# The front of layer 2: transposes one group ahead, score turns behind them, later additions on GpSimd

## The chip, the core and the metric

The kernel runs on one core of a Trainium2 chip. The core has five engines that matter here: PE (TensorE: matrix products and transposes), DVE (VectorE), ACT (ScalarE), POOL (GpSimd) and SP (SyncE, which here only issues DMAs). Each engine works through its own list of instructions in order; an instruction that waits holds up all that stand behind it in the same list. Engines wait for each other by semaphores. The metric is the device time of one execution in microseconds (us).

## What is computed

Four layers follow each other. Each adds a graph network and then a feed-forward network to `x`, an array of 2708 rows (nodes) and 256 columns in float32. The change lies at the seam between layer 1's feed-forward network and layer 2's graph network, which in the reference reads, cut to what matters:

```python
x = x + _L1_ffn_ref(...)                       # layer 1 ends
# layer 2, graph attention on the normalised rows
h = x @ W.T
a_src = (h * attn_src).sum(axis=-1)
a_dst = (h * attn_dst).sum(axis=-1)
scores = a_src[None, :] + a_dst[:, None]
mask = (adj > 0).astype(h.dtype)
s = jnp.where(scores > 0, scores, ALPHA * scores) * mask      # ALPHA = 0.2
e = jnp.exp(s - max) * mask
w = e / (e.sum(axis=1) + 1e-08)
out = elu(w @ h)
```

The kernel uses that exp of the leaky score is the larger of two products. It scales row j of `h` by exp(a_src[j]) and keeps that factor as a 257th column (together `hh`), and it needs one row of exp(0.8 a_dst) laid over all partitions (`Rb`) and one column exp(-0.8 a_src) (`G`). An element of the attention matrix is then max(Rb, G) times the mask.

## The kernel before, in words

The 2708 rows are 21 tiles of 128 and one of 20. `FOURS` splits them into six groups: one of two tiles, then five of four (the last has three full tiles and the one of 20).

Layer 1's feed-forward network has left its result in device memory (`given[1]`), written there row by row by indirect DMAs. The front of layer 2 does this for each group, with the lines of the profile:

1. SP loads the group's rows of that result into the tile `mine` (L56 in `load_tiles`; L61 for the 20 rows). `mine` has two buffers, so the third load may be issued only when the first group's additions have read theirs, and so on. Each load is 512 KB for a group of four.
2. DVE adds `mine` to `x`, two tiles at a time (L1413, 128x512).
3. PE transposes each tile of `x` in two halves into PSUM (L213 in `turn_to`), and ACT copies them to the tile `xT4` (L214, 128x256, one copy per tile). `ps_tmp` has three PSUM banks.
4. DVE takes mean and variance of each row (L186 `bn_stats`, L187), ACT makes 1/sqrt of it by logarithm and exponential (L141, `var`). The mean needs no subtraction, since the weights were centred.
5. PE multiplies by the weights and the two attention vectors (L260, 258 columns, one PSUM bank per tile; `ps_acc` has five banks).
6. ACT scales the two score columns into `sc` (L1425); GpSimd has cleared `sc` before (L1421).
7. The row scores are turned from a column to a row: a transpose on PE (L1342), a copy on ACT (L1344), a write to device memory by SP (L1345), a read by SP that lays the row over all partitions (L1349, into `Rb`), and an exponential on ACT (L141 on `Rb`). This is the round trip of the scores.
8. ACT makes the other exponentials (L141: the 257th column of `hh`, `G`, `rowe`), and DVE scales the products from PSUM into `hh` (L1433), which also frees the five `ps_acc` banks.

Behind the front comes the attention loop (L1494 on DVE makes the elements `e`, in four buffers; L1502 on PE multiplies them with `hh`). DVE makes the first four `e` while the front still runs. After each diagonal tile of `e` has been read, GpSimd copies a block into `mask` (L1781).

The order on each engine is not written out by hand here. The framework under the kernel takes the order of the calls and the dependences and puts the instructions of neighbouring groups into each engine's list as it sees fit; each engine then keeps to its list. What the engines' lists look like after the change can be read from the built program.

Of the kernel before, what the change touches and what calls it, by code (L numbers as in the profile page):

```python
# [8 lines left out]
F32 = mybir.dt.float32  # L9
# [27 lines left out]
def rows(t):  # L37
    return min(P, N - t * P)
# [8 lines left out]
FOURS = [range(0, 2)] + [range(t, min(t + 4, NT)) for t in range(2, NT, 4)]  # L47
# [19 lines left out]
def adj_ffn4(ctx: ExitStack, tc: tile.TileContext, a: dict, out: bass.AP):  # L67
# [72 lines left out]
    def lnexp(out, in_, func, **kw):  # L140
        i = s.activation(out, in_, func, **kw)  # L141
        tc.add_manual_dep(i.ins, pinned[-1].ins.name, mybir.DependencyInfo(
            mybir.DependencyClass.NoSync, mybir.DependencyReason.DATA), reason="table")
# [33 lines left out]
    def stats(tiles, src=None, by_log=False):  # L177


        G = len(tiles)  # L180
        mv = small.tile([P, G, 2], F32, name="mv", tag=f"mv{G}", bufs=2)
        v.memset(mv[:, G - 1, :], 1.0)
        for i, t in enumerate(tiles):
            r = rows(t)
            st = small.tile([P, 6], F32, name="st")
            v.bn_stats(st[:r], x[:r, t, :] if src is None else src[:r, i, :])  # L186
            v.bn_aggr(mv[:r, i, :], st[:r])  # L187
        var = small.tile([P, G], F32, name="var", tag=f"var{G}", bufs=2)
        if by_log:
            lnexp(var, mv[:, :, 1], AF.Ln, bias=eps)  # L190
            lnexp(var, var, AF.Exp, scale=-0.5)
            return mv, var
        v.tensor_scalar(var, mv[:, :, 1], EPS, None, op0=ALU.add)
        return mv, rsqrt(small, var, G)
# [14 lines left out]
    def turn_to(xT, xn, r, bank=None):  # L209

        p = ps_tmp() if bank is None else bank
        for c in range(DC):
            te.transpose(p[:, c * P : c * P + r], xn[:, c * P : (c + 1) * P], ident[:r, :r])  # L213
        s.copy(xT, p[:, : DC * P].rearrange("p (c t) -> p c t", c=DC)[:, :, :r])  # L214
# [297 lines left out]
    def behind(i, past):  # L512
        for p in past:
            tc.add_manual_dep(i.ins, p.name, mybir.DependencyInfo(
                mybir.DependencyClass.Sync, mybir.DependencyReason.DATA), reason="scattered rows")
# [822 lines left out]
    def row_scores(kept, scores, t0, n):  # L1338


        p = ps_tmp()
        te.transpose(p[:n, :P], scores, ident)  # L1342
        er = w_l1[:n, 0, :P]
        s.copy(er, p[:n, :P])  # L1344
        nc.sync.dma_start(kept.rearrange("t h c -> (t h) c")[t0 : t0 + n, :], er)  # L1345
# [16 lines left out]
    with tc.tile_pool(name="t3", reuse_waits="tile", bufs=1) as t3:  # L1362
# [34 lines left out]
        with tc.tile_pool(name="g2", reuse_waits="tile", bufs=1) as gp:  # L1397
# [2 lines left out]
            rowe = gp.tile([P, NT, 1], F32, name="rowe")  # L1400
            Rb = gp.tile([P, NT * P], F32, name="Rb")
            kept = tc.dram_tile([NT, 1, P], F32, name="rows2")
            for tiles in FOURS:
                n, t0 = len(tiles), tiles[0]
                o = gp.tile([P, 4, D], F32, name="mine", bufs=2)
                for i in load_tiles(nc, o, tiles, given[1], t0):
                    behind(i, scattered["given1"])
                for k in range(0, n, 2):
                    for q, m in (((P, 2),) if rows(t0 + k + 1) == P else
                                 ((P, 1), (rows(t0 + k + 1), 1))):  # L1410
                        i = k if q == P else k + 1
                        xs = x[:q, t0 + i : t0 + i + m, :]
                        v.tensor_tensor(xs, xs, o[:q, i : i + m, :], ALU.add)  # L1413
                xT = gp.tile([P, DC, W], F32, name="xT4", bufs=2)
                own = tiles_of(t0 * P, (n - 1) * P + rows(tiles[-1]))
                for t, k, r in own:
                    turn_to(xT[:, :, k : k + r], x[:r, t, :], r)
                rstd = stats(tiles, by_log=True)[1]

                sc = gp.tile([P, 4, 2], F32, name="sc", bufs=2)  # L1420
                g.memset(sc, 0.0)  # L1421
                ps = []
                for i, (t, k, r) in enumerate(own):
                    ps.append(times(xT, k, r, w_l2, D + 2, ps_acc()))
                    s.activation(sc[:r, i, :], ps[-1][:, D:], AF.Copy, scale=rstd[:r, i : i + 1])  # L1425
                row_scores(kept, sc[:, :n, 1], t0, n)
                row_factor(Rb[:, t0 * P : (t0 + n) * P], kept, 0, t0, n)
                lnexp(hh[:, t0 : t0 + n, D], sc[:, :n, 0], AF.Exp)
                lnexp(G[:, t0 : t0 + n, 0], sc[:, :n, 0], AF.Exp, scale=-0.8)

                lnexp(rowe[:, t0 : t0 + n, 0], sc[:, :n, 1], AF.Exp, scale=-0.2, bias=ln8)
                for i, (p, (t, k, r)) in enumerate(zip(ps, own)):
                    v.tensor_scalar(hh[:r, t, :D], p[:, :D], rstd[:r, i : i + 1], hh[:r, t, D :],  # L1433
                                    op0=ALU.mult, op1=ALU.mult)

            spread_out(hh[:, FULL, :])
            spread_out(G[:, FULL, :])
# [593 lines left out]
```

## Time and profile before

| | us |
|---|---|
| median of four runs shown | 1925.19 (1918.24 to 1929.15) |
| the profiled execution | 1930.74 |
| its span, first instruction to last | 1929.0 |
| of it: up to the first load of `mine` | 1103.62 |
| layer 2's front, to the first product of the attention loop | 36.36 (PE busy 29.11, DVE 27.52, ACT 19.08, POOL 2.88) |
| attention loop, to 1355 | 215.02 (PE busy 211.02, DVE 115.84) |
| the rest | 574.00 (PE busy 550.88) |

The profile comes from one execution. A timeline row gives the start in us, the length, the engine, the line in the kernel, the operation, the names of what is written and read, the shapes, how many equal instructions were put together, and in brackets how long the engine stood idle before it and what ended that. `PEld` rows are weight loads, which run beside the products. A group row gives the busy time, the mean length of one in ns, and the idle time before the group with its releasers. The chain of waits follows the work that ended last back from the end: each row is a start, a length, and what the time went to. "issue" is time in which the profile shows no wait.

### The profile page before, as it was taken

To read this page: it belongs to the slowest core of one execution; us is meant where nothing else is said; L and a number is where in the kernel's file an instruction comes from. 1 tells how busy PE (TensorE), PEld (TensorE's weight loads), DVE (VectorE), ACT (ScalarE), POOL (GpSimd) and SP (SyncE) were. 2 spreads that over 40 slices of the span, in tenths; PEclk is the share of its full clock that TensorE was granted. 3 is DMA by queue.
4 is the path that set the end of the run, shared out by engine and by line. 5 is a ranking of instruction groups with operands and counts; after the bars stand their busy time and mean duration, and the time that the engine had idled before them with its cause. 6 is when DMAs were issued, how large, how long until landed. Compare 5 with 4: busy or idle time off the path is not lost.

```text
span 1929.0 us, 25747 instructions
## 1 busy us (share of the span) xinstructions
PE 1832.0 (95%) x9453; PEld 1328.7 (69%) x9453; DVE 1100.7 (57%) x2498; ACT 643.1 (33%) x1459; POOL 343.2 (18%) x406
## 2 busy tenths in 40 slices
PE   7999998999999999999989699999899999999998
PEld 6888787888888888887778578888557732232344
DVE  7777861443433625344532175555354398999897
ACT  7868741222222303113222142222232552031131
POOL 1004254333322001303356300000000000000000
PEclk9999998999998999999999999999899999999999
DMA  8435655887773554544679620000101000000000
GB/s 274 137 112 162 218 187 214 316 331 276 279 290 104 171 151 118 150 114 131 201 246 341 226 68 1 1 1 1 44 1 33 17 1 23 23 12 28 20 20 15
DMA packets 90142, 243.94 MB, mean 126 GB/s; under 512 B 18160, under 2 KB 44824, under 8 KB 80793
## 3 DMA queue, kind: packets, MB, share of 16 engines
q1 hardware_dynamic: 73048, 199.80, 30.7%
q0 software_dynamic: 16960, 42.42, 6.9%
q8 instruction: 78, 1.28, 0.3%
q14 instruction: 56, 0.45, 0.1%
HBM read 216.29 MB, written 28.71 MB: 127 GB/s over the span
## 4 chain that ended last, share of the span: by engine, by line
PE 39%; DMA 4%; DVE 2%; ACT 2%; issue 2%; POOL 1%; another core or an unknown queue 0%; POOLq 0%; SPq 0%; DVEq 0%; ACTq 0%
PE num L1929 10%; PE ps_acc L1502 9%; PE den L1939 6%; PE ps_tmp L367 4%; PE ps_acc L1692 3%; PE ps_tmp L260 2%; DMA L_ffn_beta<-in_L_ffn_beta 1%; PE yacc L719 1%; PE ps_acc L260 1%; DMA names<-taken,b_ix 1%; DMA given<-ys,names 1%; PE ps_tmp L213 1%; DVE e L1899 1%; DMA wb<-in_L_ffn_Wdp 0%; DMA taken<-names,r_ix 0%
## 5 line engine op out<-in xcount | busy, mean ns | idle before, releaser
L1899 DVE SCALAR_TENSOR_TENSOR e<-arena,G,mask 128x1024 f32<-128x1024 f32 (+1 forms) x264 | 287.0, 1148 | 13.7 <-PE den L1939 13.6
L1929 PE MATMUL num<-e,wh 128*64 128x512 f32 (+4 forms) x1056 | 215.7, 551 | 0.0
L1502 PE MATMUL ps_acc<-hh,e 128*128 128x257 f32 x882 | 199.3, 382 | 1.9 <-ACT o L1445 1.9
L1290 PE MATMUL acc<-sup,adrow 128*128 128x256 f32 x882 | 200.8, 385 | 0.3 <-DVE adrow L1258 0.3
L929 PE MATMUL acc<-msg,wt 128*128 128x256 f32 x882 | 198.1, 381 | 2.8 <-DVE x L954 1.6
L1290 PEld LDWEIGHTS acc<-sup,adrow 128*128 128x128 f32 x882 | 167.1, 192 | 28.8 <-issue 5.9
L929 PEld LDWEIGHTS acc<-msg,wt 128*128 128x128 f32 x882 | 165.2, 190 | 28.7 <-DVE x L954 2.3
L1502 PEld LDWEIGHTS ps_acc<-hh,e 128*128 128x128 f32 x882 | 163.7, 190 | 29.5 <-ACT o L1445 4.5
L617 PE MATMUL yacc<-wb,hTs 128*128 128x256 f32 x736 | 171.4, 385 | 6.6 <-DVE ys L619 3.8
L583 PE MATMUL ps_acc<-xTs,wa 128*128 128x256 f32 (+1 forms) x768 | 171.4, 376 | 4.9 <-DVE xTs L573 3.8
L585 ACT ACTIVATE hTs<-ps_acc,wa 128x256 f32<-128x256 f32 (+1 forms) x192 | 88.9, 465 | 247.8 <-PE yacc L617 167.4
L583 PEld LDWEIGHTS ps_acc<-xTs,wa 128*128 128x128 f32 x768 | 137.5, 191 | 32.2 <-DVE xTs L573 7.4
L617 PEld LDWEIGHTS yacc<-wb,hTs 128*128 128x128 f32 x736 | 138.8, 193 | 26.3 <-DVE ys L619 5.0
L1929 PEld LDWEIGHTS num<-e,wh 128*64 128x64 f32 (+1 forms) x1056 | 66.5, 136 | 127.3 <-issue 105.6
L1494 DVE SCALAR_TENSOR_TENSOR e<-Rb,G,mask 128x640 f32<-128x640 f32 (+2 forms) x110 | 85.0, 773 | 90.6 <-PE ps_acc L1502 90.4
L1939 PE MATMUL den<-e,wh 128*32 128x512 f32 (+4 forms) x1056 | 118.0, 548 | 0.0
L214 ACT COPY xT<-ps_tmp 128x256 f32<-128x256 f32 x98 | 33.7, 365 | 240.4 <-PE ps_tmp L213 218.6
L1255 DVE TENSOR_SCALAR mask<-adrow 128x1024 uint8<-128x1024 f32 (+1 forms) x66 | 41.5, 629 | 123.3 <-DMA adrow<-in_adjT 122.6
L719 PE MATMUL yacc<-wb,hTs 128*128 128x256 f32 x384 | 89.6, 387 | 10.5 <-DMA wb<-in_L_ffn_Wdp 8.1
L719 PEld LDWEIGHTS yacc<-wb,hTs 128*128 128x128 f32 x384 | 72.6, 194 | 21.7 <-issue 9.6
L887 DVE SCALAR_TENSOR_TENSOR wt<-adrow,wt 128x640 f32<-128x640 f32 (+3 forms) x67 | 71.1, 1063 | 28.0 <-ACT wt L141 23.9
L1939 PEld LDWEIGHTS den<-e,wh 128*32 128x32 f32 (+1 forms) x1056 | 30.2, 108 | 77.9 <-issue 73.8
(457 smaller groups left out, 2565.9 us busy)
## 6 DMA issues: line engine op xcount, KB each, us to landing
adhalf<-in_adjT SPq DMA_DIRECT2D x42, 677.0 KB
wb<-in_L_ffn_W2p SPq DMA_DIRECT2D x24, 1152.0 KB
wb<-in_L_ffn_Wdp SPq DMA_DIRECT2D x24, 1152.0 KB
wa<-in_L_ffn_W1b SPq DMA_DIRECT2D x24, 1028.0 KB
adrow<-in_adjT SPq DMA_DIRECT2D x42, 512.0 KB
adrow<-in_adjT SPq DMA_DIRECT2D x42, 320.0 KB
adrow<-in_adjT SPq DMA_DIRECT2D x21, 576.0 KB
adrow<-in_adjT SPq DMA_DIRECT2D x21, 448.0 KB
```

Of the source, the lines that this page charges most:

```text
L367: te.matmul(p[:, :w], lhsT=w1[:, c, f * P : (f + 1) * P], rhs=xnT[:, c, c0 : c0 + w], start=(c == 0), stop=(c == DC - 1))
L583: i = te.matmul(p[:, f % 2, : m * P], lhsT=w1[:, c, f * P : (f + 1) * P], rhs=xT[:, c, : m * P], start=(c == 0), stop=(c == DC - 1))
L585: s.activation(hT[:, f, : m * P], p[:, f % 2, : m * P], AF.Gelu, bias=bias[:, f : f + 1])
L617: te.matmul(q[:, k, :], lhsT=hT[:, f, k * P : (k + 1) * P], rhs=w2[:, f, :], start=(f == 0), stop=(f == HC - 1))
L719: te.matmul(q, lhsT=hT[:, f, :], rhs=w2[:, f, :], start=(f == 0), stop=(f == HC - 1))
L929: te.matmul(p[:q, n - pair[0], :], lhsT=wt[:, k : k + q], rhs=msg[:r, j, :], start=(j == 0 and n == pair[0]), stop=(j == FULL - 1 and n == ...
L1290: te.matmul(p[:q, n - pair[0], :], lhsT=ad[:, k : k + q], rhs=sup[:, jj, :], start=(jj == 0 and n == pair[0]), stop=(jj == FULL - 1 and n ...
L1494: i = v.scalar_tensor_tensor(e[:r, :w], Rb[:r, c0 : c0 + w], G[:r, j, :], mask[:r, j, c0 : c0 + w], op0=ALU.max, op1=ALU.mult)
L1502: te.matmul(p[:, : D + 1], lhsT=e[:, k : k + q], rhs=hh[:, j, :], start=(j == 0), stop=False)
L1899: v.scalar_tensor_tensor(e[:, :w], slow[:, m % 2, k, :w], G[:, j, 2 * pair + k, :], mask[:, j, c0 : c0 + w], op0=ALU.max, op1=ALU.mult)
L1929: te.matmul(num[k * DK : (k + 1) * DK, hf, :q], lhsT=wh[some, j, 2 * pair + k, :DK], rhs=e[some, h0 - c0 : h0 - c0 + q], start=(j == 0), s ...
L1939: te.matmul(den[z : z + Q, :q], lhsT=wh[some, i, 2 * pair + k, DK : DK + 1] .to_broadcast([some.stop - some.start, Q]), rhs=e[some, h0 - c ...
```

## The change

The loop over the groups is split in two functions and run one group out of step.

`turned_up(tiles)` does steps 1 to 4 of a group: load, addition, transposes, copies, statistics. It differs in three things. Two tiles are transposed into one PSUM bank, so that one copy of 128x512 takes the place of two of 128x256. A pair is transposed right after its own addition. And from the third group on the additions are given to GpSimd (`adder`).

`valued(tiles, xT, rstd)` does steps 5, 6 and 8: products, score columns, exponentials, `hh`. The `hh` products are called ahead of two of the exponentials.

The loop at the end calls `turned_up` of the next group behind `valued` of the present one, so that the transposes of group k + 2 are called ahead of the products of group k + 1, and calls the score turns (`row_scores`, `row_factor`, step 7) behind those transposes. The first pass fills two groups.

```diff
-            for tiles in FOURS:
+
+            def turned_up(tiles):
+
                 n, t0 = len(tiles), tiles[0]
+                adder = v if t0 < FOURS[2][0] else g
                 o = gp.tile([P, 4, D], F32, name="mine", bufs=2)
                 for i in load_tiles(nc, o, tiles, given[1], t0):
                     behind(i, scattered["given1"])
+                xT = gp.tile([P, DC, W], F32, name="xT4", bufs=2)
                 for k in range(0, n, 2):
...
-                        v.tensor_tensor(xs, xs, o[:q, i : i + m, :], ALU.add)
-                xT = gp.tile([P, DC, W], F32, name="xT4", bufs=2)
+                        adder.tensor_tensor(xs, xs, o[:q, i : i + m, :], ALU.add)
+                    p = ps_tmp()
+                    for i in range(2):
+                        q = rows(t0 + k + i)
+                        for c in range(DC):
+                            te.transpose(p[:, (c * 2 + i) * P : (c * 2 + i) * P + q],
+                                         x[:q, t0 + k + i, c * P : (c + 1) * P], ident[:q, :q])
+                    s.copy(xT[:, :, k * P : (k + 1) * P + r],
+                           p.rearrange("p (c t) -> p c t", c=DC)[:, :, : P + r])
+                return tiles, xT, stats(tiles, by_log=True)[1]
+
+            def valued(tiles, xT, rstd):
+
+                n, t0 = len(tiles), tiles[0]
                 own = tiles_of(t0 * P, (n - 1) * P + rows(tiles[-1]))
-                for t, k, r in own:
-                    turn_to(xT[:, :, k : k + r], x[:r, t, :], r)
-                rstd = stats(tiles, by_log=True)[1]
...
-                row_scores(kept, sc[:, :n, 1], t0, n)
-                row_factor(Rb[:, t0 * P : (t0 + n) * P], kept, 0, t0, n)
                 lnexp(hh[:, t0 : t0 + n, D], sc[:, :n, 0], AF.Exp)
...
+                return sc, t0, n
+
+            ahead, todo = [turned_up(FOURS[0])], list(FOURS[1:])
+            for k in range(len(FOURS)):
+                sc, t0, n = valued(*ahead.pop(0))
+                while todo and len(ahead) < 2:
+                    ahead.append(turned_up(todo.pop(0)))
+                    if len(ahead) == 1:
+                        row_scores(kept, sc[:, :n, 1], t0, n)
+                if k > 0:
+                    row_scores(kept, sc[:, :n, 1], t0, n)
+                row_factor(Rb[:, t0 * P : (t0 + n) * P], kept, 0, t0, n)
```

Nothing else in the program changes. In the attention loop DVE's list has one `e` placed one step later; on the other engines the lists behind the front are the same.

More of the change, by code (lines that the diff above doesn't have):

```diff
@@ L1407, in adj_ffn4 @@
                     behind(i, scattered["given1"])
+                xT = gp.tile([P, DC, W], F32, name="xT4", bufs=2)
                 for k in range(0, n, 2):
-                    for q, m in (((P, 2),) if rows(t0 + k + 1) == P else
-                                 ((P, 1), (rows(t0 + k + 1), 1))):
+                    r = rows(t0 + k + 1)
+                    for q, m in (((P, 2),) if r == P else ((P, 1), (r, 1))):
                         i = k if q == P else k + 1
                         xs = x[:q, t0 + i : t0 + i + m, :]
-                        v.tensor_tensor(xs, xs, o[:q, i : i + m, :], ALU.add)
-                xT = gp.tile([P, DC, W], F32, name="xT4", bufs=2)
+                        adder.tensor_tensor(xs, xs, o[:q, i : i + m, :], ALU.add)
[10 more added lines that the diff above has]
+                n, t0 = len(tiles), tiles[0]
                 own = tiles_of(t0 * P, (n - 1) * P + rows(tiles[-1]))
-                for t, k, r in own:
-                    turn_to(xT[:, :, k : k + r], x[:r, t, :], r)
-                rstd = stats(tiles, by_log=True)[1]
                 sc = gp.tile([P, 4, 2], F32, name="sc", bufs=2)
@@ L1425, in adj_ffn4 @@
                     s.activation(sc[:r, i, :], ps[-1][:, D:], AF.Copy, scale=rstd[:r, i : i + 1])
-                row_scores(kept, sc[:, :n, 1], t0, n)
-                row_factor(Rb[:, t0 * P : (t0 + n) * P], kept, 0, t0, n)
                 lnexp(hh[:, t0 : t0 + n, D], sc[:, :n, 0], AF.Exp)
-                lnexp(G[:, t0 : t0 + n, 0], sc[:, :n, 0], AF.Exp, scale=-0.8)
-                lnexp(rowe[:, t0 : t0 + n, 0], sc[:, :n, 1], AF.Exp, scale=-0.2, bias=ln8)
                 for i, (p, (t, k, r)) in enumerate(zip(ps, own)):
@@ L1434, in adj_ffn4 @@
                                     op0=ALU.mult, op1=ALU.mult)
+                lnexp(G[:, t0 : t0 + n, 0], sc[:, :n, 0], AF.Exp, scale=-0.8)
+                lnexp(rowe[:, t0 : t0 + n, 0], sc[:, :n, 1], AF.Exp, scale=-0.2, bias=ln8)
+                return sc, t0, n
[9 more added lines that the diff above has]
+                row_factor(Rb[:, t0 * P : (t0 + n) * P], kept, 0, t0, n)
             spread_out(hh[:, FULL, :])
```

## The prediction

> **What bounds the kernel now.** I read the page first, then the chain of waits from 1100 us, then each engine's timeline there. On the page PE is busy 95% of the span; a stretch matters only where PE stands still in it. The changed stretch, layer 2's front, runs from the first load of `mine` (1103.62) to the first product of the attention loop (1139.98): 36.36 us, in which PE is busy 29.11, DVE 27.52, ACT 19.08. In the loop behind it PE is busy 211.02 of 215.02 us, so what the front loses or gains is passed on whole.
>
> ```profile
> span 1929.0 us, 25747 instructions
> ```
>
> The chain, start, length, what:
>
> ```profile
> 1103.62 2.66 DMA mine<-given
> ...
> 1113.26 3.50 PE ps_acc L260 x16
> ...
> 1117.78 2.70 DMA rows<-L_gnn_W
> 1120.50 3.24 DMA Rb<-rows
> 1123.73 0.02 issue
> 1123.76 0.63 ACT Rb L141
> 1124.39 0.27 ACT xT L214
> 1124.65 0.04 issue
> 1124.70 0.44 PE ps_tmp L213 x2
> ```
>
> See that a row-score round trip (write, read back, exponential) gets on the chain, because ACT's queue holds the next group's xT copies behind it. PE's timeline shows the same place and the small waits of every group (idle before, and releaser, in brackets):
>
> ```profile
> 1118.42 3.65 PE L260 MATMUL ps_acc<-w_l,xT 128*128 128x258 f32 x16
> 1122.51 0.27 PE L1342 MATMUL ps_tmp<-ident,sc 128*4 128x128 f32 x1 [0.44 <-ACT sc L1425]
> 1122.62 0.94 PE L213 MATMUL ps_tmp<-ident,x 128*128 128x128 f32 x6
> 1124.70 0.44 PE L213 MATMUL ps_tmp<-ident,x 128*128 128x128 f32 x2 [1.14 <-ACT xT L214]
> 1139.98 0.70 PE L1502 MATMUL ps_acc<-hh,e 128*128 128x257 f32 x2
> ```
>
> The rows that price what is added, from the groups of GpSimd and the timelines of GpSimd and DVE:
>
> ```profile
> L1821 POOL TENSOR_TENSOR x<-x,L_gnn_b 128x256 f32<-128x256 f32 x5 | 3.5, 721 | 368.1 <-PE ps_tmp L260 366.9 <-DVE st L186 1.2
> 1128.30 0.95 POOL L1781 COPY mask<-diag 128x128 uint8<-128x128 uint8 x1 [5.25 <-DVE e L1494]
> 1130.13 0.29 POOL L1781 COPY mask<-diag 128x128 uint8<-128x128 uint8 x1
> 1128.26 0.84 DVE L1494 SCALAR_TENSOR_TENSOR e<-Rb,G,mask 128x640 f32<-128x640 f32 x1
> 1110.74 0.69 DVE L1413 TENSOR_TENSOR x<-x,mine 128x512 f32<-128x512 f32 x1
> ```
>
> **The change, part by part.** I take prices from rows and walk them along the order in which the built program of the changed kernel lists each engine's instructions. The same walk over the kernel before puts its first loop product at 1140.1; the trace says 1139.98.
>
> *Transposes one group ahead, turns of the scores behind them.* The work of PE is the same: per group of four, 8 transposes 1.13 us (1117.30 to 1118.42), 16 product passes of 0.2175 = 3.48, one score turn 0.13. What goes are the waits: 0.44 before each of five score turns (ACT's last `sc`), and 1.14, 0.20 and 0.21 for xT copies. PE's own work sets a floor: first transposes 1107.06 to 1108.17 (clock 0.50 until 1110.25 in the windows); then, new, one transpose of the second group stands ahead of the first products and waits for DVE's add (1107.94 + 0.65), so the products start at 1108.95, three passes at half clock, five at full: 1111.3; seven transposes and the turn: 1112.45; here PE waits until about 1113 for ACT, which does eight small operations before it copies xT; 8 transposes, 16 passes, 8 transposes, turn, one product (1.13 + 3.48 + 1.13 + 0.13 + 0.87): 1119.8 to 1120.1. From there to the loop 3 x 0.87 + 1.13 + 0.13 + 3.48 + 1.05 + 0.13 + 3.48 + 0.13 + 3.48 + 0.16 (one wait for an hh) = 15.8. Floor: 1135.8, that is -4.2 us.
>
> *Copies.* 22 copies of 128x256 (1.24 per four on ACT) become 11 of 128x512 (0.535 each, L671's two in 1.07): 0.9 us less on ACT, off the path.
>
> *Round trip of the scores.* The turn now stands behind 8 transposes and its copy behind two xT copies, so rows land some 2 us later. By the walk the first exponential of Rb still waits for its data until 1120.4, but what it holds up, the fourth group's copies, is needed by PE only at 1126. The later Rb are needed by DVE's `e` from 1128, for the loop: hidden. This cover ends when the round trip takes about 0.5 us more; beyond that it costs 1 us per us.
>
> *Additions by GpSimd.* DVE loses six adds of 0.63 and three smaller: 5.1 us, not on the path. GpSimd gains seven of 128x512, one of 128x256, one of 20x256. Price a of the big one: not below the 128x256 row (0.72), not above twice it (1.44), unless stretched. A memset of 128x8 takes 0.105 there; taking 0.1 as fixed, 0.1 + 2 x 0.6 = 1.30, my value. A sentence on the page that speaks against this: the Trainium skill's GPSIMD Engine Reference (3.1) has GpSimd at about 2.6 cycles per element of a two-input add and advises VectorE; worked out from that, a would be about 1.2 us, an estimate, and the main loop would start about 0.5 us earlier than by my row, so the advice alone does not make the change a loss.
>
> The added wait sits in DVE's queue: there the `bn_stats` of the last group's first pair stand ahead of the second group's four `hh` products, and they wait for GpSimd's adds. Those hh products free the ps_acc banks that the third group's second product needs. The ladder: third `mine` lands by 1110.74 (row above; issued 1107.03, so 3.71); two adds; only then may SP issue the fifth load (two buffers), 3.71; two adds; the first of the last group (its load is in by then); 0.05; two bn_stats 0.66; one hh 0.53; 0.05 to PE. That is 1110.74 + 3.71 + 1.29 + 5a = 1115.74 + 5a, 1122.24 at a = 1.30. PE has been ready since 1120.0 and stands about 2.2 us. Loop start 1122.24 + 15.8 = 1138.0, **2.0 us earlier**. In general 1131.5 + 5a: -1.3 at 1.44, the floor's -4.2 from a = 0.86 down, equal to before at 1.69.
>
> What else queues on GpSimd: the memsets of `sc` for groups four to six stand behind the adds (last add about 1122.4) and ACT needs the first of them at 1127; the mask copies come after 1128 as before. SP: the score rows' first write stands behind the fifth load, as in the trace (issue 1112.57, read-back only at 1116.45), and Rb's first read behind the last load: both are in the 1120.4.
>
> *Can the adds be stretched?* Bounds: the mask copy took 0.29 alone and 0.95 beside DVE's `e` (two operands in SBUF), ending 0.15 after it: +0.66. The five adds of L1821, beside bn_stats and products read from PSUM, stayed at 0.72. In the new order DVE has only bn_stats, aggregates and hh products (from PSUM) between 1110.7 and 1122.4, so I take nothing; the other end, +0.66 on each, is a = 1.96 and +1.4 us. The Trainium skill's SBUF — State Buffer ("Who interferes with whom") says the same of two-input VectorE operations against GpSimd reads, as an exclusive lock, and by it the stretch is nothing as well.
>
> Sum: -2.0 us. The profiled execution took 1930.74 (span 1929.0 and 1.7 around it), 5.5 over the median 1925.19 of the runs shown; the difference carried to the median gives 1923.2. A measurement of this kernel can tell about 0.5% (9.6 us) from no change.
>
> **The rivals.**
> *Packed PE.* If a is 0.86 or less, nothing stands ahead of PE: -4.2, 1921.0. For it: a memset of 128x1024 takes 0.95 there. Against: L1821 reads two operands and takes 0.72 for half the elements.
> *Slower: GpSimd's adds pace the front.* Each 0.1 us on a costs 0.5; from a = 1.69 the loop starts later than before; at 1.96 1926.6; at 3.6 it would pass 0.5%. For it: the 0.95 copy. Against: no two-input DVE operation is in that stretch.
> *The round trip stays.* If rows and Rb land 1 us later than in the trace, the walk gives about -1, 1924.2. For it: loads of `mine` share SP's queue. Against: from the fourth load on the queue is nearly empty.
> *Nothing.* The waits removed and the one added cancel: 1925.2.
>
> **How the numbers follow.** Likeliest (0.5 to 3.5 us off): 0.57, 1923.2. Packed: 0.16. Round trip: 0.06. Nothing: 0.06. Slower: 0.15. All of them lie within 0.5%: the whole floor is 4.2 us, 0.22%. What passes the bound is spread between runs, or adds of 3.6 us: 0.05 faster, 0.05 slower, 0.90 within. The mechanisms span 1921 to 1926.6; the runs of one kernel here span -7 to +4 around their median, so a median can lie some 4 to 5 off: 1916.5 to 1929.5.
>
> **What would show it.** Right: five score turns without a wait for `sc`; no xT wait of 1 us; one wait of about 2 us at the third group's second product, released by DVE hh; bn_stats of the last group waiting for GpSimd; adds of 1.3 us; first loop product near 1138.0. Wrong: adds above 1.69 or uneven, PE waits in several groups, a loop start after 1140, or a loop of more than 215 us.

## The result and the profile after

The changed kernel took 1922.01 us (median of 50 runs, 1915.33 to 1934.06), the kernel before beside it 1922.96 us (median of 78 runs, 1918.14 to 1934.00). The ratio is 0.9995, with a 95% interval of 0.9988 to 1.0002: no difference that this measurement can tell, and at most 2.3 us gained or 0.4 us lost. The prediction was 1923.2 us in a range of 1916.5 to 1929.5, with a chance of 0.90 for "within 0.5%".

The profiled execution of the changed kernel took 1919.55 us. Its page begins with:

```profile
span 1917.8 us, 25727 instructions
```

That span is 11.2 us below the 1929.0 of the profile before, and most of this is not the change. The first load of `mine` begins at 1094.97 in place of 1103.62: 8.65 us were won ahead of the front, in code that the change doesn't touch. That point moves without the change too: in four profiles from one chip below (kernel before, again; changed kernel, again; turns first; first split) it lies between 1077.96 and 1083.80. So the comparison has to be made stretch by stretch. Two windows of the trace of before and the same two of after, the front (first load of `mine` to the first product of the loop) and the loop; the columns are length, then busy time and instructions of PE, PE's weight loads, DVE, ACT and GpSimd, then the granted clock, the DMA share and GB/s:

```profile
1103.62:1139.98 36.36, 29.11 (x138) 21.64 (x138) 27.52 (x83) 19.08 (x79) 2.88 (x10) 0.91 0.34 110
1139.98:1355.00 215.02, 211.02 (x1042) 175.19 (x1041) 115.84 (x273) 56.43 (x214) 6.22 (x20) 1.00 0.01 2
```

```profile
1094.97:1129.52 34.55, 29.04 (x137) 22.93 (x138) 23.66 (x74) 17.87 (x68) 12.78 (x19) 0.85 0.35 113
1129.52:1344.50 214.98, 210.96 (x1042) 175.23 (x1041) 116.02 (x273) 56.83 (x214) 6.17 (x20) 1.00 0.01 3
```

The front went from 36.36 to 34.55 us: 1.81 us less, where the prediction had 2.0. PE is busy as long as before (29.04 against 29.11); what went is waiting. GpSimd's busy time rose from 2.88 to 12.78 us, DVE's fell from 27.52 to 23.66. The loop is unchanged (214.98 against 215.02), so the gain is passed on, and not taken back later. Only the clock column is worse: 0.85 on the mean of the front, 0.91 before.

The chain of waits in the front of after (start, length, what):

```profile
1094.97 2.68 DMA mine<-given
...
1098.40 3.72 DMA mine<-given
...
1102.19 2.51 POOL x L1417 x2
...
1104.72 3.69 DMA mine<-given
...
1108.47 3.74 POOL x L1417 x3
...
1112.91 0.54 DVE hh L1440
...
1113.50 2.88 PE ps_acc L260 x12
```

This is the ladder that the prediction wrote down: third load, two additions, the fifth load into a buffer that they set free, three additions, two `bn_stats` (left out here), one `hh`, and only then the third group's products. The `rows` and `Rb` transfers, which stood on the chain before, are gone from it.

PE's timeline in after (start, length, what; idle before it and its releaser in brackets):

```profile
1100.10 0.47 PE L1422 MATMUL ps_tmp<-ident,x 128*128 128x128 f32 x1 [0.56 <-DVE x L1417]
1100.37 3.80 PE L260 MATMUL ps_acc<-w_l,xT 128*128 128x258 f32 x8
1110.89 0.27 PE L1342 MATMUL ps_tmp<-ident,sc 128*4 128x128 f32 x1
1113.50 2.88 PE L260 MATMUL ps_acc<-w_l,xT 128*128 128x258 f32 x12 [1.46 <-DVE hh L1440]
1129.52 0.70 PE L1524 MATMUL ps_acc<-hh,e 128*128 128x257 f32 x2
```

The score turns (L1342) now have no bracket: their wait of 0.44 us is gone. The new wait, 1.46 us, is the one that was foreseen, at the place that was foreseen. The eight product passes of the first group took 3.80 us. In the trace of before they took 3.04, because there the clock came up to full speed 3.3 us after the first transposes, and here only 7.2 us after them:

```profile
1108.20 3.04 PE L260 MATMUL ps_acc<-w_l,xT 128*128 128x258 f32 x8
```

From the timelines of GpSimd and DVE in after:

```profile
1102.19 2.50 POOL L1417 TENSOR_TENSOR x<-x,mine 128x512 f32<-128x512 f32 x2 [6.94 <-DMA mine<-given]
1108.47 5.08 POOL L1417 TENSOR_TENSOR x<-x,mine 128x512 f32<-128x512 f32 x5 [0.98 <-DMA mine<-given]
1112.24 0.75 DVE L186 BATCH_NORM_STATS2 st<-x 128x6 f32<-128x256 f32 x2 [0.20 <-POOL x L1417]
```

Two additions of 128x512 take 2.50 us, so one takes 1.25 (predicted 1.30); a single record is 1.27 long. The row of five holds three of them, one of 128x256 and one of 20x256. They keep their length beside `bn_stats` and `hh`: nothing stretches them. The `bn_stats` of the last group's first pair wait for GpSimd, and the `hh` that PE needs follow in DVE's queue.

### The profile page after: what moved, and what is told of

Same layout as the page of the kernel before. It is cut to its first block, busy times and chain, and to the rows that moved or that the text cites. A ratio compares the mean times of both kernels' runs of the same rounds, so it can differ in the third digit from the quotient of the medians.

```text
span 1917.8 us, 25727 instructions
## 1 busy us (share of the span) xinstructions
PE 1827.9 (95%) x9453; PEld 1327.9 (69%) x9453; DVE 1095.6 (57%) x2489; ACT 641.9 (33%) x1448; POOL 352.4 (18%) x415
## 4 chain that ended last, share of the span: by engine, by line
PE 38%; DMA 4%; DVE 4%; issue 2%; ACT 1%; POOL 1%; DVEq 0%; SPq 0%; POOLq 0%; ACTq 0%
PE num L1951 10%; PE ps_acc L1524 9%; PE den L1961 5%; PE ps_tmp L367 4%; PE ps_acc L1714 3%; PE ps_tmp L260 2%; DVE e L1921 1%; PE yacc L719 1%; DMA L_ffn_beta<-in_L_ffn_beta 1%; DMA given<-ys,names 1%; DMA wb<-in_L_ffn_Wdp 1%; PE ps_acc L260 1%; DMA mine<-given 1%; DMA hs<-hid,names 1%; PE ps_tmp L213 0%
## 5 line engine op out<-in xcount | busy, mean ns | idle before, releaser
L214 ACT COPY xT<-ps_tmp 128x256 f32<-128x256 f32 x76 | 26.9, 367 | 219.4 <-PE ps_tmp L213 218.1
L887 DVE SCALAR_TENSOR_TENSOR wt<-adrow,wt 128x640 f32<-128x640 f32 (+3 forms) x67 | 71.1, 1063 | 26.8 <-ACT wt L141 21.3
```

## The experiments

The theory under test: *the ladder of GpSimd's additions and of the two `mine` buffers ends last in the front; behind it lies a floor set by PE.* The rivals: the clock (half speed for longer than before) sets the front; the round trip of the scores still sets it; the buffers or DVE do. The measure is the front, first load of `mine` to first product of the loop. Times of whole runs come from several chips, whose levels differ by up to 15 us, so each ratio is to runs of the kernel before on the same chip.

**All additions back on VectorE.**

```diff
-                adder = v if t0 < FOURS[2][0] else g
+                adder = v
```

> The changed kernel with one part undone: all additions of the front stay on VectorE, none goes to GpSimd. Measure: the front in the profile, from the first load of mine to the first product of the loop; it was 36.36 us before and 34.55 after.
> Ladder theory (the pace of GpSimd's additions and the two mine buffers set the one stall in TensorE, 1.46 us before the third group's second product): the third group's hh comes earlier, that stall falls below 0.3 us, and the front is bounded by TensorE: the 31.10 us from the first transposes to the loop after the change, less 1.46 and up to 1 us more where the queue runs fuller, so a front of 32.0 to 33.2 us, and 1.4 to 2.5 us off the whole against the changed kernel, a ratio to the kernel before of about 0.998.
> Rival, the clock (half speed for 7.1 us after the first transposes after the change, 3.2 us before): the stall would then only change its place, TensorE being late anyway, and the front stays within 0.5 us of 34.55.
> Rival, VectorE: 9 additions of 0.63 us go back into VectorE's queue, 5.7 us in all, and stand ahead of the bn_stats and hh behind them; if VectorE has no room for them the stall grows and the front is 36 us or more.

Measured: 1905.93 us beside 1908.78; ratio 0.9984 (0.9970 to 0.9998). PE's timeline of this run:

```profile
1088.72 0.48 PE L1422 MATMUL ps_tmp<-ident,x 128*128 128x128 f32 x1 [0.49 <-DVE x L1417]
1099.62 3.65 PE L260 MATMUL ps_acc<-w_l,xT 128*128 128x258 f32 x16
1116.42 0.70 PE L1524 MATMUL ps_acc<-hh,e 128*128 128x257 f32 x2
```

The third group's 16 passes now run through, without the wait. The front, from 1083.61, is 32.81 us, inside the 32.0 to 33.2 of the ladder theory, 1.74 below the changed kernel's 34.55. The clock rose 6.3 us after the first transposes here, hardly sooner than in after (7.2), so the clock is not what held the front of after. DVE, busy 27.48 us of 32.81, had room for the additions.

**Each GpSimd addition twice.** Ahead of each addition GpSimd makes it once more into a tile that nobody reads.

```diff
+            idle = gp.tile([P, 2, D], F32, name="idle")
...
+                        if adder is g:
+                            g.tensor_tensor(idle[:q, :m, :], xs, o[:q, i : i + m, :], ALU.add)
                         adder.tensor_tensor(xs, xs, o[:q, i : i + m, :], ALU.add)
```

> The changed kernel with each GpSimd addition made twice: ahead of each real one GpSimd adds the same two operands into a spare tile that nobody reads, so that the price of an addition on GpSimd goes from 1.26 us to about 2.5 us and nothing else is changed. The output is the same.
> Ladder theory, by the prediction's formula for the start of the loop, 1131.5 + 5a on the axis of the trace of before: at a = 2.52 it is 1144.1, which makes the front 40.5 us, 6 us more than the 34.55 measured after the change, and the stall ahead of the third group's second product 7 to 8 us, or less there and the rest ahead of later groups; a ratio to the kernel before of about 1.002.
> Rivals (TensorE packed, or the clock, or the scores' round trip sets the end): only the slack is eaten, the front grows by less than 2 us, and the ratio stays within 0.999 to 1.001.
> A price between, 2 to 3 us for the whole front, would mean that the ladder is there but is climbed fewer times than the formula says.

Measured: 1912.33 us beside 1908.78; ratio 1.001 (0.9994 to 1.0026). The front is 43.08 us, 8.5 above after, more than the 6 expected. Out of the chain of this run:

```profile
1091.49 1.27 POOL idle L1419
...
1092.83 1.27 POOL x L1420
...
1107.32 0.54 DVE hh L1443
...
1107.90 5.53 PE ps_acc L260 x12
```

The chain has become GpSimd alone, from 1091.49 to 1106.96 without a load in it, because two doubled additions outlast a load. `hh` lets PE go 20.80 us after the first transposes (1087.10), 5.7 later than in after: that is the ladder. The other 2.7 are in the last line: twelve passes take 5.53 us here and 2.88 in after. During PE's wait of 4.40 us the granted clock fell to 0.50, and it stayed there until 1113.7. The front grew by 6.3 to 6.7 us against the kernel before, which would be a ratio of 1.0034; the measured one is smaller. The profiled execution was the longest of the ten (1917.06 us), so the median execution may have lost less in the front, or won time elsewhere. This stays open.

**Additions made dearer by half.** The same, with a smaller addition (one tile, 128x256) in front:

```diff
+                            g.tensor_tensor(idle[:q, 0, :], x[:q, t0 + i, :], o[:q, i, :], ALU.add)
```

> The changed kernel with each GpSimd addition preceded by a smaller one that nobody reads (one tile, 128x256, of the same operands into a spare tile): the price of a step goes from 1.26 to about 2.05 us. The output is the same.
> The chain of the changed kernel is: third load landed, two additions, fifth load (3.7 us), three additions. From 1.85 us a step on, two steps last longer than the load, and the load leaves the chain. Ladder theory: hh ready 17.0 to 18.9 us after the first transposes (15.1 before the edit), a stall of 3.4 to 5.3 us, a front of 36.2 to 38.5 us, which is that of the kernel before (36.4 and 36.8) or longer: the break-even of the prediction, 1.69 us an addition, is passed. If TensorE stands for more than 3.4 us and the clock falls as with the doubled additions, up to 3 us more.
> Rival (only the doubled price was enough to reach the path): the front stays below 35.5 us.

Measured: one run of 1927.47 us beside 1923.43. PE's timeline at the wait:

```profile
1118.90 5.41 PE L260 MATMUL ps_acc<-w_l,xT 128*128 128x258 f32 x12 [3.93 <-DVE hh L1443]
```

PE was let go 17.70 us after the first transposes (1101.20), in the span of 17.0 to 18.9 that the chain gives; the wait is 3.93 (3.4 to 5.3 expected). The clock fell here too, the twelve passes took 2.53 us longer than in after, and the front was 39.74 us, 3.0 and 3.4 above the two profiles of the kernel before. So at some 2 us an addition the order of the change is a loss, of which the wait alone accounts for 0.4 to 0.9 us and the fallen clock for the rest.

**Four buffers for `mine`, additions still on GpSimd.**

```diff
-                o = gp.tile([P, 4, D], F32, name="mine", bufs=2)
+                o = gp.tile([P, 4, D], F32, name="mine", bufs=4)
```

> The changed kernel with four buffers for mine in place of two, the additions where the change put them: the load of the third and of later groups no longer waits for a GpSimd addition to free a buffer.
> Ladder theory: of the ladder's terms the 3.7 us of reissue and landing between the second and the third load's users goes, and the five additions that stand one behind another do not all stand behind the load any more; the stall falls from 1.46 to 0.3 to 0.5 us and the front from 34.55 to about 33.5 us (33.2 to 33.9).
> Rival (the buffers are not in the ladder, only the additions' own time is): stall and front stay within 0.3 us of 1.46 and 34.55.
> Rival (the loads collide when they start at once; the four loads take 2.7 to 3.7 us each in the trace after): the first additions come later and the front grows by 0.5 us or more.

Measured: 1907.27 us beside 1908.78; ratio 0.9995 (0.9977 to 1.0014). The wait before the third group is gone and the front is 33.75 us (expected 33.2 to 33.9): the buffers are a rung of the ladder. It is not all gain, since the loads now go out together: the second group's landed 4.89 us after its start and PE waited 1.65 us for its addition, 0.56 in after. PE's timeline, at that wait and at the third group's passes:

```profile
1089.81 0.47 PE L1422 MATMUL ps_tmp<-ident,x 128*128 128x128 f32 x1 [1.65 <-DVE x L1417]
1100.55 3.65 PE L260 MATMUL ps_acc<-w_l,xT 128*128 128x258 f32 x16
```

**The additions alone, in the order of before.**

```diff
-                        v.tensor_tensor(xs, xs, o[:q, i : i + m, :], ALU.add)
+                        (v if t0 < FOURS[2][0] else g).tensor_tensor(xs, xs, o[:q, i : i + m, :], ALU.add)
```

> The kernel before with one part of the change alone: the additions from the third group on by GpSimd; order, turns and copies as before.
> Ladder theory: without the group ahead TensorE waits for each group's chain anyway, and an addition of 1.26 us on GpSimd stands in that chain in place of 0.63 us on VectorE wherever it is not covered: the front is 36.4 to 38 us, 0 to 1.6 us longer than the 36.36 before, a ratio of 1.000 to 1.001.
> Rival (GpSimd's additions relieve VectorE, which is 83 percent busy in the front before): the front gets shorter than 36 us.

Measured: 1910.53 us beside 1908.78; ratio 1.0017 (0.9997 to 1.0037). The front is 37.96 us, 1.2 to 1.6 above before: relieving DVE, which the rival counted on, is worth nothing there. Out of the chain:

```profile
1089.28 3.43 DMA rows<-L_gnn_W
...
1092.78 2.94 DMA Rb<-rows
```

The scores' round trip is still on the chain, as in the kernel before. So the gain of the change comes from the order of PE's and ACT's work, and the additions on GpSimd take part of it away.

**Score turns ahead of the next transposes again.** Everything else as in after.

```diff
                 sc, t0, n = valued(*ahead.pop(0))
+                row_scores(kept, sc[:, :n, 1], t0, n)
                 while todo and len(ahead) < 2:
                     ahead.append(turned_up(todo.pop(0)))
-                    if len(ahead) == 1:
-                        row_scores(kept, sc[:, :n, 1], t0, n)
-                if k > 0:
-                    row_scores(kept, sc[:, :n, 1], t0, n)
```

> The changed kernel with its second part undone: each group's score turn is called ahead of the next group's transposes again, the transposes still run a group ahead, the additions stay on GpSimd.
> Ladder theory: the turn's wait for the scores (0.44 us each before the change) comes back only where TensorE has no slack; of up to 0.44 us for each of five groups most is taken out of the stall of 1.46 us or hidden: a front of 34.4 to 35.5 us.
> Rival (the turns behind the transposes are what brought the gain of 1.8 us): the front is 36 us or more.

Measured: one run of 1906.61 us; the front is 37.90 us, 3.2 above after. My expectation failed and the rival was right: the turns behind the transposes are needed for the gain, though more than half of the 3.2 us came by the clock. ACT's timeline shows why, and PE's what it costs:

```profile
1093.80 0.26 ACT L1437 ACTIVATE sc<-ps_acc,var 128x2 f32<-128x2 f32 x1 [0.61 <-PE ps_acc L260]
1097.19 0.42 ACT L141 ACTIVATE Rb<-Rb 128x256 f32<-128x256 f32 x1 [3.13 <-DMA Rb<-rows]
1097.51 0.24 ACT L1437 ACTIVATE sc<-ps_acc,var 128x2 f32<-128x2 f32 x1
```

```profile
1097.81 0.27 PE L1342 MATMUL ps_tmp<-ident,sc 128*4 128x128 f32 x1 [2.31 <-ACT sc L1437]
1099.03 5.00 PE L260 MATMUL ps_acc<-w_l,xT 128*128 128x258 f32 x14
```

I had priced only PE's wait of 0.44 us per turn. But a turn called earlier brings `Rb`'s exponential forward in ACT's queue as well: it now stands between two of the second group's `sc` copies and blocks ACT for 3.13 us until `Rb` has landed, and the turn that needs the second of these copies waits 2.31 us on PE. In after all four `sc` stand ahead of that exponential, which waits only 0.86 us and holds up nothing that PE needs soon. The sum: 1.5 us more of waits on PE than in a second run of after (0.82 + 0.44 + 2.31 + 0.29 against 0.47 + 0.35 + 1.56), and 1.8 us because fourteen passes take 5.00 in place of 3.21 us, the clock having fallen to half for 3.4 us, 1.3 us after the wait had ended.

**The kernel before and the changed kernel again,** for the clock and for how well the front repeats.

> The kernel before, once more, for its front and for the clock. In its first profile TensorE's granted clock came up 3.2 us after the first transposes; in the four kernels of the first experiments 6.1 to 7.0 us after them, also in the one that has the order of before (6.3).
> Theory (the moment is set by something that runs free of this program's order): the delay is anywhere between 3 and 7.5 us here, and the front moves less than 0.5 us with it, because TensorE of before waits for other things in its first 8 us: 36.0 to 36.9 us from the first load of mine to the loop.
> Rival (the change's new idle 0.56 us ahead of the first products keeps the clock down): 3.2 us again.
> Rival (the clock sets the front of before): at 6 to 7 us the front is 37.5 us or more.

> The changed kernel, once more, beside the next one. Ladder theory: the stall ahead of the third group's second product is 1.46 us less what TensorE is later or more what it is earlier by the clock, and the sum is the same: hh ready 15.0 to 15.2 us after the first transposes and a front of 34.3 to 34.9 us, whatever the clock does. If the clock sets the front, a delay of 3 us in place of 7.1 makes it 33 us.
> The ratio to before: 0.998 to 1.000.

> The changed kernel, a third time, as the partner of the run above on the same chip. Front 34.3 to 34.9 us, stall ahead of the third group's second product 1.3 to 2.3 us by the clock, ratio to before 0.997 to 1.0005.

Measured: before 36.78 us of front, with the clock up 6.1 us after the first transposes (first profile: 36.36 and 3.3). After 34.66 and 34.81, with 6.1 and 5.0 us (first: 34.55 and 7.2); waits ahead of the third group 1.56 and 1.84 us. So the front repeats within 0.5 us and the change is worth 1.6 to 2.2 us of it. In the third profile of after the printed chain leaves the ladder at the `hh` that lets PE go and follows ACT's copy to the round trip of the scores; but `hh` began 0.67 us after the pair of `bn_stats` that waited for GpSimd, as in the other two, so the ladder ended the wait there as well. The delay of the clock is not the change's doing, since the kernel before shows 6.1 as well, and neither front depends much on it. The ratios of these two sets of runs of after are 0.9978 (0.9967 to 0.9988, 1907.13 beside 1911.31 us) and 1.0000 (0.9983 to 1.0016, 1922.43 beside 1923.43); with the first, 0.9995, they lie around the 0.999 that 1.9 of 1920 us make.

**The first group turned tile by tile, the second group's transposes held behind the first products;** first with the additions on VectorE.

```diff
-                adder = v if t0 < FOURS[2][0] else g
+                adder = v
...
+                    if t0 == 0:
+                        for i in range(2):
+                            turn_to(xT[:, :, i * P : (i + 1) * P], x[:, i, :], P)
+                        continue
                     p = ps_tmp()
...
+                            if t0 == FOURS[1][0]:
+                                tc.add_manual_dep(nc.cur_bb.bb.instructions[-1], firsts[-1],
+                                                  mybir.DependencyInfo(
+                                    mybir.DependencyClass.NoSync, mybir.DependencyReason.DATA),
+                                    reason="order")
...
+                    if t0 == 0:
+                        firsts.append(nc.cur_bb.bb.instructions[-1].name)
```

> All additions on VectorE as in the first experiment, and the first group (two tiles) turned tile by tile as before the change, with the second group's transposes held behind the first group's products: the idle 0.49 us ahead of the first products should go.
> Theory (TensorE is now the bound from its first products on): the front, 32.81 us in the first experiment, falls by 0.3 to 0.8 us, to 32.0 to 32.5; a ratio to before of 0.9975 to 0.9985, about 0.001 below the changed kernel's.
> Rival (behind the first products TensorE waits for the second group's copies anyway, 0.16 us in the first experiment): the wait only moves there, and the front stays at 32.6 to 33.0 us.

> All additions on VectorE and the first group turned tile by tile, once more, beside the changed kernel. In its first run the clock came up 3.27 us after the first transposes and the front was 31.55 us; the first experiment's kernel, without the second edit, had 6.28 and 32.81.
> Theory A (the clock's delay depends on nothing that these kernels do in the front): the delay may be 3.3 or 6 to 7 here; at 6 to 7 the front is 32.0 to 32.4, at 3.3 it is 31.4 to 31.7.
> Theory B (the first products following the transposes without a gap bring the clock up early): 3.2 to 3.4 us again.
> The ratio to the kernel before: 0.996 to 0.998, below the changed kernel's beside it by about 0.001.

Measured: fronts of 31.55 us (clock up after 3.3; below the 32.0 to 32.5 expected) and 32.10 us (after 5.6); 1904.55 beside 1911.31 us, ratio 0.9967 (0.9954 to 0.9981), and 1919.28 beside 1923.43 us, ratio 0.9976 (0.9960 to 0.9993). In each pair it lies below the changed kernel, by 0.0011 and 0.0024, though the intervals of a pair overlap. By its front this version beats both: 4.3 to 5.2 us less than before, 2.5 to 3.3 less than after. PE's timeline of the second run:

```profile
1100.38 1.11 PE L213 MATMUL ps_tmp<-ident,x 128*128 128x128 f32 x4 [10.31 <-DVE x L1418]
1101.52 3.81 PE L260 MATMUL ps_acc<-w_l,xT 128*128 128x258 f32 x8
1129.04 0.70 PE L1536 MATMUL ps_acc<-hh,e 128*128 128x257 f32 x2
```

Between its first line and its last PE's timeline has not one more bracket: PE is packed, and the front is PE's own work plus 3.4 us of load and first addition. The first run has one wait, at the place that the rival named:

```profile
1093.15 0.66 PE L1427 MATMUL ps_tmp<-ident,x 128*128 128x128 f32 x4 [0.77 <-ACT xT L1434]
```

So in the first run the edit only moved the waits of the first experiment (0.49 and 0.16 us) to here, and what its front fell further came almost all from the earlier clock; in the second run the edit took them away. Between the two runs the later clock made the first eight passes and the next eight transposes 1.2 us longer, and 0.6 of that went out of the wait for ACT: that leaves the 0.55 us between 32.10 and 31.55. Of the two theories on the rise, B fails: the second run had 5.6 us with the same order.

**The same with the additions on GpSimd.** Only the `adder` line is the change's own again.

> The first group turned tile by tile and the second group's transposes held, as in the run of that name, but with the additions on GpSimd as the change has them.
> Ladder theory: TensorE gets to the third group's second product 0.4 to 1.3 us earlier and waits that much longer there (1.9 to 2.8 us); the front stays at 34.3 to 34.9 us. Nothing ahead of the stall is worth anything while the ladder stands.
> Rival (the stall is only one of several bounds of like size): the front falls by half of the gain or more, below 34.0 us.

Measured: one run of 1920.21 us beside 1923.43; the wait is 2.17 us (1.9 to 2.8 expected), and PE was let go 15.16 us after the first transposes, as in after (15.08, 15.17, 15.14). Nothing ahead of the ladder moves it. But the front is 36.41 us, not 34.3 to 34.9. PE's timeline, and windows ahead of, in and behind the slow stretch (the granted clock is the third column from the end):

```profile
1112.49 4.57 PE L260 MATMUL ps_acc<-w_l,xT 128*128 128x258 f32 x12 [2.17 <-DVE hh L1452]
```

```profile
1109.90:1113.31 3.41, 1.24 (x6) 0.76 (x6) 3.11 (x11) 1.67 (x5) 2.70 (x5) 1.00 0.04 11
1113.31:1116.72 3.41, 3.41 (x10) 2.67 (x9) 1.68 (x9) 0.80 (x4) 0.00 (x0) 0.50 0.25 77
1116.75:1118.00 1.25, 1.25 (x12) 1.15 (x11) 0.37 (x1) 0.88 (x5) 0.00 (x0) 1.00 0.00 0
```

PE reached the ladder earlier, waited 0.6 us longer than in its sister run, and the clock was halved for 3.4 us, from 0.8 us after it had begun to work again. The twelve passes took 1.69 us more than in after, which is the whole miss (36.41 against the 34.66 of the second run of after is 1.75; the sums of PE's waits, 2.36 and 2.38, are alike).

## Why the prediction was right

It was right by its steps, and two of its sizes were off in ways that cancelled. That the time came out within 0.5% says little about them, since the largest gain that it weighed was 4.2 us, 0.22%; the front shows them. The terms, in us, with the three profiles of after (the fifth load from the first two):

| term | predicted | measured |
|---|---|---|
| one addition on GpSimd | 1.30 | 1.25 to 1.27 |
| fifth load, from issue to landing | 3.71 | 3.69, 3.73 |
| PE let go, after the first transposes | 15.18 | 15.08, 15.17, 15.14 |
| PE ready there | 12.94 | 13.62, 13.61, 13.30 |
| the wait | 2.2 | 1.46, 1.56, 1.84 |
| from there to the loop | 15.8 | 16.02, 16.02, 16.02 |
| the front | 34.4 | 34.55, 34.66, 34.81 |
| change of the front | -2.0 | -1.8, and -1.6 to -2.2 over all pairs |

*Transposes ahead, turns behind.* The waits of 0.44 for the scores and of 1.14, 0.20 and 0.21 for the copies went, as said. The floor of -4.2 us, which the prediction said lay behind the ladder, is there: with the additions on VectorE the front is 3.6 us shorter than in the first profile of before, and with the first group's copies split 4.3 and, where the clock rose early, 4.8. What the prediction had wrong is the walk up to the wait: it took the clock of the trace of before, up 3.2 us after the first transposes, and it rose after 5.0 to 7.2. PE was therefore ready 0.4 to 0.7 us later than the prediction said. That cost nothing, since PE would have waited for the ladder anyway, and it shortened the wait by as much. That the two errors cancelled is the ladder's doing; that the shortened wait left the clock at full speed was luck (last section).

*From the wait to the loop.* 16.02 in place of 15.8: the 60 passes took 13.72 us by the chain, 13.05 by the row that I took (the last group's 16 passes took 3.80 in place of 3.48 in the trace of before already); the 16 transposes 1.75, where I had 2.18.

*Copies:* off the path, as said. *Round trip:* hidden in after, as said, with a wait of 0.86 us at ACT that reached nobody. The prediction named 0.5 us more as the end of that cover. No run made the round trip longer. By the rows of after, the copies behind that exponential end at 1113.23 and PE comes to the next transposes, which need the banks that they free, at 1116.22: the cover was about 3 us, an estimate. What the prediction did not say is that the second part of the change provides it: without that part PE waited 1.5 us more, and with the fallen clock the front was 3.2 us longer.

*Additions on GpSimd.* The ladder stands as written, and its price too: 1.25 to 1.27. From the addition of 128x256 in the row of L1821 (0.72) to one of 128x512 (1.27 by its record) it is 0.55 us, which leaves 0.17 fixed: the prediction's 0.6 and 0.1 were each a little off and near in the sum. The Trainium skill's GPSIMD Engine Reference (3.1), weighed in the prediction, has about 2.6 cycles per element; for 512 elements at its 1.2 GHz that is an estimate of 1.11 us, and the trace agrees for the part that grows with the length, 2 x 0.55 = 1.10. The formula of five additions held at this price only: from 1.85 us an addition on, two of them outlast the load, and the load leaves the chain, so that PE was let go at 17.70 and 20.80 us where the formula gives 18.7 (at 2.0) and 21.3 (at 2.52). The break-even of 1.69 was not met exactly by a run; at 2.0 the order lost 3.0 to 3.4 us, 2.5 of them by the clock.

*Stretching:* none, as said. The seven additions of 128x512 are all 1.26 to 1.29 us long in the three profiles, with DVE's `bn_stats` and `hh` beside them. A DVE operation with two operands in SBUF did not run beside them, so the other end of that range was not put to the test.

*The whole.* -2.0 us against 1925.19, the median of four runs, made 1923.2. The larger set puts the kernel before at 1922.96 and the change at -0.95 us, with an interval of -2.3 to +0.4; two further sets give a ratio of 0.9978 and 1.0000. The front's 1.9 us are shown by the profiles. That the whole time falls by as much, a ratio of 0.9990, lies inside two of the three intervals and just above the third (0.9967 to 0.9988): it is consistent with the runs, and not more than that.

*The rivals.* "Packed PE" did not occur in after, and is what the kernel becomes when the additions go back to VectorE. "GpSimd's adds pace the front" is the state of after, on the winning side of its break-even. "The round trip stays" was wrong for after; each half of the change alone had the round trip on the path again: additions without the order (37.96 us), and order without the late turns (37.90, of which 1.8 by the clock). "Nothing" is wrong for the front; the whole time cannot tell it from the forecast.

## What to carry to other kernels

When waits are removed ahead of a bound engine, write down the chain that then ends last, with the price of each rung; here the additions' move to GpSimd, which relieved an engine that was not on the path, gave back 1.7 to 2.0 of the 3.6 to 4.0 us that the new order was worth. Price a moved step in every queue that it shifts: the score turn looked like 0.44 us on PE and was 1.5 us of waits, through the exponential that follows it into ACT's queue, and 1.8 us of slow clock behind them. And of two kernels with the same sum of waits, the one that has them in a single piece may pay for the clock as well.

## What the runs showed of the hardware that was not expected

*A wait of about 2 us can halve PE's clock, and where it falls in time decides.* After waits of PE of 1.46, 1.56 and 1.84 us in the front the granted clock stayed at 1.00. After 2.17, 2.31 (and 0.29 soon after), 3.93 and 4.40 us it was at 0.50, for 3.4, 3.4, 6.8 and 6.8 us. In the shortest case it fell 0.8 us after PE had begun to work again. The price was 1.69, 1.8, 2.53 and 2.65 us on top of the wait. The length alone does not decide: ahead of the front in the first profile of before a wait of 2.89 us, from 1064.40 on, left the clock at 1.00. In each of the 14 traces all changes of the granted clock lie whole multiples of 3.413 us apart (in after from 1105.59 to 1344.52, for example, 70 of them). Cut into steps of 3.413 us at these moments, the traces have 74 steps at full clock in which PE stood for 2.02 us or more in all, and behind every one of them the clock was at half; no step with more than 1.95 us kept it. With less it was mostly kept, though not always: 29 of the falls came behind such a step. The wait of 2.17 us lay in one step (the first window shown with the last experiment). So did that of 1.84, and the 2.89 us were split by a step's end into 1.55 and 1.34:

```profile
1112.74:1116.15 3.41, 1.57 (x11) 1.09 (x9) 2.83 (x12) 2.04 (x8) 3.41 (x5) 1.00 0.12 39
1116.15:1119.56 3.41, 3.41 (x20) 3.02 (x21) 2.45 (x11) 1.43 (x9) 0.02 (x1) 1.00 0.15 56
```

```profile
1062.54:1065.95 3.41, 1.86 (x13) 1.47 (x11) 0.00 (x0) 1.07 (x2) 2.80 (x3) 1.00 0.96 301
1065.95:1069.37 3.42, 2.07 (x10) 1.87 (x11) 0.78 (x2) 0.00 (x0) 0.54 (x2) 1.00 0.99 398
```

The Trainium skill's page TensorE: Matmul & The Clock Gate (Part 1) has the clock fall after at least one idle window of some 3.4 us. The length of the steps agrees with that; but here a step in which PE was busy 1.24 of 3.41 us ended in a fall, so the window needn't be idle throughout. The prediction's own wait of 2.2 us was long enough to halve the clock if it had come to lie in one step: the late rise of the clock at the start, which the prediction had missed, kept the wait below that in all three profiles of after.

*The clock's rise is not fixed to the work.* In the fronts it came 3.3 to 7.2 us after the first transposes, in one kernel (before) once after 3.3 and once after 6.1, in another (additions on VectorE, first group split) after 3.3 and 5.6. It came at the end of the first step of 3.413 us in which PE was busy for 2.97 us or more; steps with up to 2.91 did not bring it. Two windows of after show the rise, at the latest moment seen:

```profile
1098.42:1105.50 7.08, 6.51 (x21) 5.06 (x21) 5.50 (x21) 2.85 (x11) 3.06 (x3) 0.50 0.52 161
1105.50:1106.00 0.50, 0.50 (x6) 0.41 (x5) 0.50 (x3) 0.30 (x1) 0.50 (x1) 0.91 0.37 86
```

So a walk that takes the moment from one profile carries an error of up to 4 us of half clock. Where PE waits anyway it costs nothing, as in the kernel before and after; where PE is nearly packed it cost about 0.5 us.
